# A four-layer graph network on one core: each kind of operation gets its own shift in the planned order

## The chip, the cores and the metric

The kernel runs on one core of a Trainium2 chip. The metric is the device time of one execution in microseconds (us), given as the median of several. The core has a matmul engine (TensorE, in the profile PE, with PEld for the loading of its stationary operand), a vector engine (VectorE, DVE), a scalar engine (ScalarE, ACT), a general engine (GpSimd, POOL) and a queue engine (SyncE, SP), which here issues every DMA. Each engine works through its own instructions in the order in which the program lists them, and waits on semaphores where one needs what another engine has made.

## The reference

128 graphs of 64 nodes with 512 features each: x is (128, 64, 512) and goes through four layers, all with the same 64 x 64 adjacency. Each layer is added to its input and normalized.

```
x = layernorm(x + gnn(x))        # out = deg * (x Wi + b) + adj @ (x Wj)
x = layernorm(x + gat_ffn(x))    # 4 heads, elu, a fifth attention over W_out, elu,
                                 # relu(out @ w1 + b1) @ w2 + b2 + out, layernorm with gamma, beta
x = layernorm(x + gat2(x))       # Wh = x W; e = src_i + dst_j; leaky relu; mask; softmax; attn @ Wh
x = layernorm(x + gat3(x))
```

In a graph attention a score for each pair of nodes (e) is made from two numbers per node (f), masked, turned into weights by a softmax, and these weights average the nodes' rows.

## The kernel before

**Tiling.** The 8192 rows are cut into 32 pairs of two tiles of 128 rows (T = 2, NP = 32); a tile holds two graphs. Every pair passes through the stages of all four layers, and several pairs are under way at a time, each in another layer: a new one is begun every TURN. The names in the profile carry no pair number, but in the text axp_5_1 is pair 5, tile 1.

**Stages.** `stage_first` (line 844) aggregates x over the adjacency on PE (axp, with `aggr` as the moving operand, 64 rows of the array at a time), ACT copies the result to ax, and the product with the first layer's weight follows (l for the first four pairs, stx_0/sty_0 later); POOL adds the row degb = deg * b to x. `stage_scores` (894) makes the heads' scores: for pairs 0 and 1 by PE from x1T (fp), later by DVE's row products j. Its attention (`attention_heads`, 732) is a chain: dg on DVE, bc on PE, the softmax with e on DVE and ACT, the transposition pt on PE, the copies aT on ACT. Then come the four groups yp of eight matmuls (two halves q of the heads, two tiles), again with 64 rows each, and ACT's copies ys; POOL makes the differences t1, t2 of ys and one into ys itself. `stage_heads` (964) multiplies ys with the four heads' weights (stx_h, sty_h) into hT, with elu after it. `stage_project` (1001) multiplies hT with W_out in two halves (stx_o, sty_o) into who. `stage_out` (1041) has the fifth attention (names with 1o; op applies it, in 64 x 64 tiles), the transposition oTp, the two products of the feed-forward part (hidp, then stx_y and sty_y) and the norm with gamma (ng). `stage_gat` (1095) is run for the third and the fourth layer (bc, e, pt, then gp, the copies gT, and stx/sty with W2 or W3); `stage_last` and `stage_tile` do the last pair tile by tile, with plain products (yp of w_last, z) in places.

**Products.** `seven` and `strassen` (611, 663) compute a 2 x 2 block product with seven block products instead of eight. Each is a short unbroken group of matmuls into one of two accumulators: stx (x in the code) or sty (y and z). Their weights are blocks and differences of blocks (11, 21, 12, 22, T1 to T4), read by SP into rings of buffers, ws (4) for two weights and wk (6) for the others.

**The order.** Calls on `nc` aren't emitted but recorded: `Plan.note` (220 and around) makes a `Step` for each call, or for each group within `together()`, with a rank, which is the number in which it was recorded, less 1000 within `soon()`. `Plan.order` then lists the steps by a simulation of its own: for each engine it takes, among the steps whose inputs are there by its own cost estimates, the one with the lowest rank. SLACK and WAIT say how long after its end another engine sees a step. `Plan.play` emits the instructions in that order. So all instructions carry the line of `play` (L314), and a rank matters only against other steps that are ready on the same engine at the time. Buffers are given out in the order of recording, so a step that is to open a buffer waits for an earlier one's to come free. The steps are recorded by a queue of generators, each `yield` giving a stage's next due time.

Of the kernel before, what the change touches and what calls it, by code (L numbers as in the profile page):

```python
# [39 lines left out]

WAIT = 0.2
NEAR = 160
SLACK = {"tensor": 0.8, "sync": 0.4}


class Slots:


    def __init__(self, n):
        self.free, self.queue = [(0.0, i, None) for i in range(n)], []  # L50
        self.openers = []
# [26 lines left out]
class View:  # L78
# [48 lines left out]
    def real(self):  # L127
        a = self.tile.make()
        for name, args, kw in self.steps:
            a = getattr(a, name)(*args, **kw)  # L130
        return a
# [10 lines left out]
class Step:  # L142
    def __init__(self, engine, rank):
        self.engine, self.rank = engine, rank
        self.calls, self.after, self.behind, self.port = [], set(), set(), False
        self.opens, self.uses = [], set()
        self.takes, self.lands = 0.0, 0.0


class Plan:  # L150
# [23 lines left out]
    def note(self, engine, name, args, kw):  # L174
        if self.joined:
            s = self.joined[0]
            assert s.engine == engine
        else:
            s = Step(engine, len(self.steps) - self.early)
            self.steps.append(s)  # L180
            if self.joined is not None:
                self.joined.append(s)
        out = [kw[k] for k in ("out", "accum_out") if k in kw] + (
            [] if "out" in kw or not args else [args[0]]
        )
        views = [(v, True) for v in out if isinstance(v, View)] + [
            (v, False)
            for v in [*args, *kw.values()]
            if isinstance(v, View) and not any(v is o for o in out)
        ]  # L190
        for v, writes in views:
            t = v.tile
            writes = writes or t.pool.space is PSUM
            if not t.seen:
                s.opens.append(t)
            else:
                s.behind.add(t.seen[0][0])
            s.uses.add(t)
            s.after.update(o for o, r, w in t.seen if (w or writes) and v.meets(r))
            t.seen.append((s, v.region, writes))  # L200
        s.after.discard(s)
        s.behind -= {s} | s.after
        s.calls.append((name, args, kw))
        takes, s.lands = cost(engine, name, args, kw, out)
        if engine in ("vector", "gpsimd"):

            both = [v for v, writes in views if not writes and v.tile.pool.space is not PSUM]
            s.port = len(both) > 1 and (engine == "vector" or size_of(out) > 2)
        s.takes += takes

    def order(self):
# [21 lines left out]
        def late(s, e):  # L233
            return 0.0 if s.engine == e else WAIT + SLACK.get(s.engine, 0.3)

# [73 lines left out]
    def play(self):  # L309
        real = lambda v: v.real() if isinstance(v, View) else v  # L310
        with self.tc.manual_schedule():
            for s in self.order():
                for name, args, kw in s.calls:
                    getattr(getattr(self.tc.nc, s.engine), name)(  # L314
                        *map(real, args), **{k: real(v) for k, v in kw.items()}
                    )
# [10 lines left out]
def size_of(out):  # L327
    return max(math.prod(v.shape[1:]) for v in out) if out and isinstance(out[0], View) else 512


def cost(engine, name, args, kw, out):

    size = size_of(out)
    if engine == "tensor":
        if name == "transpose":
            return size * 0.00085, 0.0

        beside = P * P // math.prod(kw["lhsT"].shape)
        return (
            size * 0.00169 if beside == 1 else 0.208 / beside + 0.0003 * size  # L340
        ), 0.0
    if engine == "sync":
        return 0.06, 0.0015 * size
    if name == "tensor_tensor_reduce":
        return 0.7, 0.0
    if engine == "gpsimd":
        return 0.2 + 0.0021 * size, 0.0
    return 0.17 + (0.0011 if engine == "vector" else 0.00085) * size, 0.0
# [1001 lines left out]
```

## Time and profile before

| | us |
|---|---|
| median of three runs | 3346.63 |
| lowest, highest | 3344.84, 3348.06 |
| the profiled execution | 3347.62 |
| its span (first to last instruction) | 3345.8 |
| PE busy within it | 3284.4 |
| DVE, POOL, ACT busy | 2420.4, 1684.7, 1363.8 |

The profile is that of one execution; 1.8 us of its time lie outside the span, and it took 1.0 us longer than the median. PE's busy time counts an instruction as busy from its start to a modelled end; a stretch of busy PE therefore says that it was never without work, not that the work was done as fast as it could be. Most matmuls leave two records in the trace: the x8 of a line stands for four matmuls. The time of a group is read from its start to the start of the next. L314 stands for all of the program; the groups are told apart by the names of their tiles, first the one that is written, then those that are read.

The twelve costliest rows of the page are matmuls and weight loads of the block products, ACT's copies of hT and DVE's row products; no single row has more than a fifth of the span.

### The profile page before, as it was taken

The page shows a single profiled execution, that of the slowest core. Times are in us where ns is not written, and L with a number is a line of the kernel's source. Part 1 is how long each engine was busy: PE and PEld are TensorE (multiplying, and loading weights), DVE is VectorE, ACT ScalarE, POOL GpSimd, SP SyncE. Part 2 cuts the span into 40 slices and gives each one's busy share as a digit, 9 for nine tenths or more (in the row PEclk, how much of TensorE's full clock was granted, in tenths as well). Part 3 has the DMA queues.
Part 4 walks back from the last instruction along what each step waited for, and adds up shares of the span by engine and source line. Part 5 has one row for each costly group of instructions (what it writes and reads, how often), then busy time and mean ns, then how long its engine had stood idle before and what let it go on. Part 6 is the DMA issues. An engine that isn't in the chain of part 4 may idle for free.

```text
span 3345.8 us, 59820 instructions
## 1 busy us (share of the span) xinstructions
PE 3284.4 (98%) x21298; PEld 2888.7 (86%) x21298; DVE 2420.4 (72%) x5698; ACT 1363.8 (41%) x3196; POOL 1684.7 (50%) x1860
## 2 busy tenths in 40 slices
PE   8999999999999999999999999999999999999997
PEld 4888888988988988989888989889889889888884
DVE  5477677777777777777777777777777777777756
ACT  2444344444444443443443443434444444444332
POOL 6745345554455554455554555544555544555442
PEclk9999999999999999999999999999999999999998
DMA  8956656667666666666666666676666666666752
GB/s 309 323 168 199 216 197 215 214 212 235 203 216 218 215 215 224 200 224 215 217 226 213 200 224 218 210 232 204 209 220 216 217 228 201 217 217 208 243 183 66
DMA packets 301062, 718.08 MB, mean 215 GB/s; under 512 B 32560, under 2 KB 41824, under 8 KB 300768
## 3 DMA queue, kind: packets, MB, share of 16 engines
q1 hardware_dynamic: 300768, 714.27, 64.9%
q8 instruction: 171, 2.80, 0.3%
q14 instruction: 123, 1.01, 0.1%
HBM read 680.82 MB, written 33.32 MB: 213 GB/s over the span
## 4 chain that ended last, share of the span: by engine, by line
PE 93%; DVE 2%; DMA 2%; POOL 2%; issue 1%; ACT 0%; SPq 0%; POOLq 0%; DVEq 0%
PE stx_h L314 13%; PE stx_o L314 13%; PE stx L314 12%; PE sty_h L314 10%; PE sty_o L314 10%; PE sty L314 9%; PE hidp L314 5%; PE yp L314 4%; PE gp L314 3%; PE stx_y L314 3%; PE sty_y L314 2%; PE axp L314 2%; PE bc L314 1%; DMA rows<-d_h 1%; PE op L314 1%; PE l L314 1%
## 5 line engine op out<-in xcount | busy, mean ns | idle before, releaser
L314 DVE CUSTOM_DVE_ANT_0 j<-x,rows 128x512 bf16<-128x512 f32 x736 | 627.9, 853 | 53.5 <-DMA rows<-d_h 23.0
L314 PEld LDWEIGHTS stx_h<-ys,wh 128*128 128x128 f32 x3072 | 392.0, 192 | 16.3 <-issue 0.9
L314 PE MATMUL stx_h<-ys,wh 128*128 128x128 f32 x3072 | 404.7, 275 | 1.1 <-DVE r_1o L314 0.8
L314 ACT COPY hT<-stx_h 128x256 f32<-128x256 f32 x384 | 142.9, 373 | 480.1 <-PE stx_h L314 335.8
L314 POOL TENSOR_SCALAR rs<-mv 128x1 f32<-128x1 f32 x256 | 70.8, 277 | 501.9 <-DVE mv L314 492.0
L314 ACT ACTIVATE x<-x,sh,rs 128x512 f32<-128x512 f32 x256 | 209.1, 817 | 203.8 <-DVE sh L314 202.9
L314 PE MATMUL sty_h<-ys,wh 128*128 128x128 f32 x2048 | 274.0, 277 | 2.8 <-ACT hT L314 2.8
L314 POOL TENSOR_TENSOR ys<-ys,t 128x256 f32<-128x256 f32 x128 | 114.5, 896 | 302.2 <-PE sty_h L314 302.0
L314 PEld LDWEIGHTS sty_h<-ys,wh 128*128 128x128 f32 x2048 | 249.6, 192 | 7.9 <-ACT hT L314 3.7
L314 PE MATMUL stx_o<-ws_wo_T,s_o 128*128 128x256 f32 x1024 | 246.1, 383 | 3.6 <-ACT who L314 2.7
L314 PE MATMUL sty_o<-ws_wo,hT 128*128 128x256 f32 x1024 | 242.4, 380 | 2.5 <-DMA ws_wo<-d_wo 2.5
L314 PE MATMUL hidp<-oT,w 128*128 128x256 f32 (+1 forms) x1056 | 231.1, 373 | 0.0
L314 DVE TENSOR_TENSOR hT<-sty_h,hT 128x256 f32<-128x256 f32 x256 | 107.9, 422 | 150.1 <-PE sty_h L314 146.8
L314 PEld LDWEIGHTS hidp<-oT,w 128*128 128x128 f32 x1056 | 193.5, 190 | 24.9 <-issue 0.5
L314 PEld LDWEIGHTS sty_o<-ws_wo,hT 128*128 128x128 f32 x1024 | 190.0, 190 | 27.1 <-DMA ws_wo<-d_wo 2.7
L314 DVE TENSOR_TENSOR x<-stx,x 128x256 f32<-128x256 f32 x360 | 149.2, 420 | 87.1 <-PE stx L314 83.6
L314 PEld LDWEIGHTS stx_o<-ws_wo_T,s_o 128*128 128x128 f32 x1024 | 186.0, 191 | 28.8 <-ACT who L314 3.6
L314 DVE SCALAR_TENSOR_TENSOR hT<-elu,hT 128x512 f32<-128x512 f32 x256 | 174.8, 684 | 40.6 <-ACT elu L314 37.1
L314 ACT ACTIVATE elu<-hT 128x512 f32<-128x512 f32 x256 | 153.7, 601 | 70.0 <-DVE hT L314 66.7
L314 DVE BATCH_NORM_STATS2 st<-x 128x6 f32<-128x512 f32 x256 | 177.0, 691 | 5.5
L314 ACT COPY ys<-yp 128x512 f32<-128x512 f32 x256 | 131.7, 600 | 114.1 <-PE yp L314 113.2
L314 DVE TENSOR_TENSOR x<-sty,x 128x512 f32<-128x512 f32 (+1 forms) x180 | 100.1, 556 | 87.2 <-PE sty L314 84.1
(201 smaller groups left out, 7719.3 us busy)
## 6 DMA issues: line engine op xcount, KB each, us to landing
ws_wo_T<-d_wo_T SPq DMA_DIRECT2D x256, 512.0 KB, 3.7
ws_wo<-d_wo SPq DMA_DIRECT2D x192, 512.0 KB, 3.9
ws_W_T<-d_W_T SPq DMA_DIRECT2D x248, 256.0 KB, 3.6
rows<-d_h SPq DMA_DIRECT2D x240, 256.0 KB, 4.7
ws_w_T<-d_w_T SPq DMA_DIRECT2D x112, 512.0 KB, 3.3
ws_W<-d_W SPq DMA_DIRECT2D x186, 256.0 KB, 3.7
ws_w<-d_w SPq DMA_DIRECT2D x84, 512.0 KB, 4.1
rows<-d SPq DMA_DIRECT2D x128, 256.0 KB, 4.8
```

Of the source, the lines that this page charges most:

```text
L314: getattr(getattr(self.tc.nc, s.engine), name)(*map(real, args), **{k: real(v) for k, v in kw.items()})
```

## The change

SLACK of the matmul engine goes from 0.8 to 0.691. Each step gets a kind when its first call is recorded: two letters of its engine, and the name of the tile that it writes without the numbers ("te:bc": a matmul into a bc). Before the order is made, `play` adds to a step's rank what the table LATER has for its kind, and for its kind in its part of the program: S is the first 11% of the recorded steps, E the last 7%, M the rest (for which the table has no entry). A positive number sends a step behind others that are ready, a negative one ahead. The table has 26 entries for 23 kinds on the four computing engines and SP. No operation is added, removed or changed.

```diff
-SLACK = {"tensor": 0.8, "sync": 0.4}
+SLACK = {"tensor": 0.691, "sync": 0.4}
+LATER = {
+    "gp:bones/S": 40, "gp:fill": 120, "gp:rs": -20, "gp:s_o": -20, "gp:s_o/E": -20, "gp:ys": 8,
+    "sc:x": 100, "sy:w/S": 20, "te:bc": -60, "te:bc_o": 40, "te:fp": -12, "te:hidp": 18,
+    "te:hidp/S": 20, "te:l": -21, "te:pt/E": 9, "te:pt_o/E": -20, "te:stx/S": 80,
+    "te:stx_y/E": 80, "te:stx_y/S": 60, "te:sty_o/E": 4, "te:wap": -100, "ve:abd/S": 23,
+    "ve:deg": 40, "ve:gT/E": -100, "ve:ng": 200, "ve:who/S": -40,
+}
...
         self.calls, self.after, self.behind, self.port = [], set(), set(), False
+        self.kind = ""
...
         s.calls.append((name, args, kw))
+        if not s.kind:
+            what = out[0].tile.args.get("name", "?") if out and isinstance(out[0], View) else "dram"
+            what = re.sub("__+", "_", re.sub(r"\d+", "", what).rstrip("_"))
+            s.kind = f"{engine[:2]}:{what}"
...
         with self.tc.manual_schedule():
+            n = len(self.steps)
+            for i, s in enumerate(self.steps):
+                when = "S" if i < 0.11 * n else "E" if i > 0.93 * n else "M"
+                s.rank += LATER.get(s.kind, 0) + LATER.get(f"{s.kind}/{when}", 0)
             for s in self.order():
```

## The prediction

> **What bounds the kernel now.** I read the page first, then the waits of the matmul engine, then busy time by windows, then the timeline of one steady pair and of the places with gaps. The page:
>
> ```profile
> span 3345.8 us, 59820 instructions
> PE 3284.4 (98%) x21298; PEld 2888.7 (86%) x21298; DVE 2420.4 (72%) x5698; ACT 1363.8 (41%) x3196; POOL 1684.7 (50%) x1860
> ...
> PEclk9999999999999999999999999999999999999998
> ...
> PE 93%; DVE 2%; DMA 2%; POOL 2%; issue 1%; ACT 0%; SPq 0%; POOLq 0%; DVEq 0%
> ```
>
> PE is idle for 3345.8 - 3284.4 = 61.4 us in all, and the chain of waits runs on PE for 93% of the span. Nothing but PE's own time and these 61 us can be won. The windows (PE busy, weight loads, DVE, ACT, POOL, granted clock, DMA share, GB/s) say where the idle time lies:
>
> ```profile
> 0.00:107.00 107.00, 91.95 (x444) 54.58 (x445) 59.63 (x131) 31.37 (x60) 70.39 (x73) 0.92 0.89 313
> ...
> 428.00:535.00 107.00, 103.46 (x711) 92.09 (x713) 78.45 (x187) 46.25 (x109) 53.58 (x62) 0.98 0.60 195
> 535.00:636.20 101.20, 101.20 (x671) 90.34 (x669) 71.10 (x177) 43.11 (x101) 50.88 (x56) 1.00 0.69 223
> ...
> 3210.00:3346.00 136.00, 107.27 (x486) 78.75 (x484) 82.31 (x231) 39.84 (x108) 39.33 (x64) 0.90 0.36 120
> ```
>
> The first five windows of 107 us have about 30 us of idle PE, the last 136 us have 28.7, and the 2675 us between have 2.9. There a pair takes 101.2 us with PE full. So the middle can only become shorter if the same matmuls take less PE time. The waits (total, times, longest) name what is late at both ends:
>
> ```profile
> PE pt L314 <- DVE e L314: 8.2, 5, 4.3
> PE bc L314 <- DVE dg L314: 5.7, 1, 5.7
> PE abd_ps L314 <- DVE abd L314: 4.9, 1, 4.9
> ...
> PE sty_h L314 <- ACT hT L314: 2.8, 5, 0.7
> ...
> PE sty_o L314 <- DMA ws_wo<-d_wo: 2.5, 1, 2.5
> ```
>
> The first is the attention's DVE chain, the third the first microseconds, the fourth the only wait of the middle. PE's timeline in a steady pair (start, length, matmuls):
>
> ```profile
> 1033.67 1.24 PE L314 MATMUL stx_o<-ws_wo_T,s_o 128*128 128x256 f32 x5
> 1034.84 2.06 PE L314 MATMUL yp<-aT,x 64*128 64x128 f32 x32
> 1036.82 1.13 PE L314 MATMUL stx_y<-ws_w_T,hid 128*128 128x256 f32 x4
> 1037.79 1.89 PE L314 MATMUL sty_o<-ws_wo,hT 128*128 128x256 f32 x8
> 1039.61 2.06 PE L314 MATMUL yp<-aT,x 64*128 64x128 f32 x32
> 1041.60 1.16 PE L314 MATMUL sty_h<-ys,wh 128*128 128x128 f32 x8
> ```
>
> Each matmul leaves two records, and lengths overlap, so starts are to be subtracted. Elsewhere four stx_y records go from start to start in 0.86 and eight sty_o in 1.73. Beside a yp group stx_y takes 36.82 to 37.79 = 0.97, and sty_o ahead of one 37.79 to 39.61 = 1.82. One group of eight axp matmuls (1026.64 to 1027.73) takes 1.09, two groups of eight yp (1034.84 to 1036.82) 1.98, four of them unbroken (from 436.57 in the timeline) 3.77. With 0.89 for a group, each fits n x 0.89 + 0.20. So one unbroken segment of 64-row matmuls costs 0.10 on the way in, 0.20 inside, 0.10 on the way out: about 0.40 us, however long it is.
>
> **What the Trainium skill says.** "TensorEngine Tiling (Array Packing)", section "Tiling Modes", states "Mode switching requires drain". yp, axp and op use 64 rows, all else 128; the 0.40 above is this trace's price of it. "TensorE: Matmul & The Clock Gate", Part 1 on the HAM clock gate, has the array's clock fall to half after an idle window of some 3.4 us. The trace agrees in kind, and already at shorter gaps: after the gap of 4.25 us at 430.87 eight records of sty take 2.78 instead of 1.73, the next eight 2.46. "SBUF — State Buffer", section on its two sides, says that DVE with two SBUF inputs and GpSimd lock each other out. In the first 90 us a DVE sh of 0.16 us lasted 2.29 beside a POOL addition. "Perfetto Trace Analysis", section "Identifying the Most-Contended Engine", warns that PE's busy share is not its efficiency: here too PE is "full" while the segments cost time in it.
>
> **The change part by part.** The instructions of each engine are the same in kind and number; only their order changes. Put side by side, the two orders give four effects.
>
> 1. *Merged yp segments.* A pair has four yp groups of eight matmuls (stage_scores' aggregation). Before, they stand in two segments for 27 pairs, as in the timeline, and in 66 segments in all; after, with bc 60 ranks earlier, hidp 18 later and POOL's subtraction into ys 8 later, in one for 28 pairs, and in 38 in all. axp (60) and op (33, then 32) stay. 28 x 0.40 = -11.2 us, of it 0.4 in each steady pair, so 100.8 there.
>
> 2. *Start, 0 to 107 us.* deg and degb come before aggr on DVE, so the first axp no longer starts at 6.18 but when b0's DMA is in. That took 6.3 us from its issue at 4.03; now it stands ahead of the w0 tiles on SP, so 7.6 to 10.3, plus 0.5 for degb, plus aggr: 9.3 to 10.5, or +3.1 to +4.3 on PE. PE then runs through to 59.8, where it waits 2.12 for wap_h, which hangs on the chain of weight sums (POOL, DVE, DMA), not on PE, and loses 2.1 us at half clock afterwards. That covers the delay: PE arrives later at the same wait. At the next gap (5.68 before bc at 89.74, chain of x_1's norm) fp and bc change places and dg stands behind other work: -1 to +1. I take 0, with -2 to +4.
>
> 3. *Early pairs, 107 to 535 us.* Distances in PE work between what hands to DVE and what waits for it: bc_3_0 to pt_3_0 3.52 before, 7.82 after; pt_3_0 to gp3_0 0 and 2.62; pt_3_1 to gp3_1 0 and 3.46. The gaps at these places (1.16, 0.73, 0.84) go: -2.7. For the 4.25 gap before pt at 430.87, `ng` 200 ranks later takes foreign instructions out of the e_1_4 chain on DVE: 16 of 5.76 us before, 8 of 3.41 after (-2.35), and 0.87 us more PE work lies between: -3.2 of 5.1 (with the 0.85 gap ahead of it), and some -1.5 of the half clock's 1.8. wo0's T tiles are loaded earlier on SP: the 0.90 gap at 136 goes. The 2.73 at 192 stays (the copy of who is still behind elu on ACT). Sum -8.3; I take -8, with -2 to -11, as each new place could have its own wait.
>
> 4. *Tail, 3210 to 3346.* stx_o and sty_o stand so that the 2.45 us wait for ws_wo at 3218 has 0.8 us more work ahead of it: -1. The first yp of the last pair stands earlier, pulling that tile's attention by 2 to 3 us, but oTp of pair 31 stands nearer its o (a possible wait of 1 to 1.5). After gp the two orders are nearly the same, and the chain bc, e, pt, gp of DVE and PE stays. -2.5, with +2 to -7.
>
> The rest of the middle moves without a price as long as distances suffice. The shortest one: the last ys-dependent product. Before, 4.40 us of PE work lie between the first yp half and sty_h of head 0; merged, 1.81. ACT's four copies take 0.55 to 0.6 each and start 1.16 after the first yp, so the fourth ends 3.4 after it; sty_h stands at 3.76. Slack 0.35 us. The other rings keep their distances (ws tiles 9.8 us of PE work from slot to use, wk 5.3; loads took 3.3 to 4.1). sty_h's five waits of the middle behind hT (2.8 in all), which follow late row loads, may go or grow: 0, with -3 to +3.
>
> Sum: -11.2 + 0 - 8 - 2.5 + 0 = -21.7. The span becomes 3345.8 - 21.7 = 3324.1. The profiled run was 3347.62, 1.8 above its span and 1.0 above the median: 3324.1 + 1.8 - 1.0 = 3324.9, so 3325.
>
> **The rivals.**
> *A: only the segments count.* Start and tail are chains over several engines: what is taken out of one wait is late at the next (the 2.73 at 192 and the tail's chain are unchanged). -11.2 and -1: 3334. For it: chains through DVE are only moved; against: the 4.25 gap has 2.35 us of other DVE work in it that does go.
> *B: the ends recover in full.* -11.2, early -11, start -2, tail -7, and three of the small waits: -34, so 3312. For it: the half clock after gaps, which makes each shortened gap count nearly twice; against: the later axp at the start.
> *C: slower.* ACT isn't free when yp begins. One norm (x, 0.81 us) and one ax copy (0.57) ahead of the ys copies make the fourth late by 0.81 + 0.57 - 0.35 = 1.0; with a second norm 1.8 us. For 28 pairs at 1.8, +50 - 22 = +28: 3375; at the 1.0, +6: 3353. It decides from 21.7 / 28 = 0.8 us a pair. For it: ACT's timeline in this pair shows a norm at 1032.21 and ax copies to 1034.1, right ahead; against: ACT was then idle for 1.90 us before the first ys, and is busy for 41%. Taken at 3356.
> *D: nothing.* Half of the gain of 1 given back in waits of a quarter of a microsecond and the ends as before: about 3342. The order of the middle does change on all engines, so "not done" is excluded; a balance isn't.
>
> **How the numbers follow.** Forecast 0.50 (its own range 3317 to 3331), A 0.23, B 0.13, D 0.08, C 0.06. Two runs of this kernel can't tell less than 0.2%, 6.7 us, from no change, so faster is below 3339.9 and slower above 3353.3. Forecast, A and B are faster, with a little of D: 0.88. Most of D and a part of C are the same: 0.07; the rest of C: 0.05. The range 3309 to 3341 leaves out C, most of D and the far side of B, about 0.15.
>
> **What would show it.** Right: yp x64 in one segment of 3.77 in the steady pairs and a period near 100.8; first axp at 9 to 10.5 with wap_h's gap gone or below 1; no gap of 4 us near 430; about 45 us of idle PE in place of 61. Wrong: gaps before sty_h on ACT's ys in each pair (C); a period still at 101.2, which would mean that the 0.40 isn't a price of the segment; gaps moved, not gone, in the first 535 us (A); a wap_h gap that stays after a later axp (+4).

## The result, and the profile after

The changed kernel takes 3316.47 us (median of four runs, 3314.83 to 3322.36) against 3347.35 us for the kernel before (four runs too, 3344.84 to 3350.77), a ratio of 0.991 with a 95% interval of 0.9893 to 0.9927. The forecast was 3325 us with a range of 3309 to 3341: the result lies inside the range, 8.5 us below the forecast. The span of the profiled execution went from 3345.8 to 3313.0 us, 32.8 us less where the forecast's sum was 21.7.

The page of the kernel after, its first lines and the chain of waits by engine:

```profile
span 3313.0 us, 59778 instructions
PE 3266.4 (99%) x21298; PEld 2886.0 (87%) x21298; DVE 2491.0 (75%) x5698; ACT 1362.8 (41%) x3196; POOL 1714.9 (52%) x1860
...
PE 94%; DMA 3%; DVE 1%; POOL 1%; SPq 1%; issue 0%; ACT 0%; POOLq 0%; DVEq 0%; ACTq 0%
```

Idle PE fell from 61.4 to 3313.0 - 3266.4 = 46.6 us: 14.8 us of the gain are waits that are gone. The other 18.0 us are busy PE that became shorter, with the same matmuls. This is the split of one execution. The run without deg (below) has the same order but for one short DVE instruction in the first 5 us, so it is in effect a second profile of the changed kernel: a span of 3312.7 us, and 10.2 and 22.9 us in place of 14.8 and 18.0.

Where the 32.8 us lie is read from windows that are cut at the same work in both kernels: at the start of yp of the pairs 6, 28 and 30. Columns: window and its length, busy time of PE, weight loads, DVE, ACT and POOL (with instructions), granted clock, DMA share, GB/s. First the kernel before:

```profile
0.00:630.00 630.00, 599.87 (x3789) 506.12 (x3789) 421.70 (x981) 245.61 (x563) 335.37 (x349) 0.98 0.70 233
630.00:2860.10 2230.10, 2228.05 (x14677) 1989.32 (x14676) 1657.68 (x3894) 930.23 (x2178) 1130.80 (x1255) 1.00 0.66 216
2860.10:3063.60 203.50, 202.78 (x1335) 180.81 (x1334) 151.44 (x354) 84.48 (x198) 103.05 (x115) 1.00 0.67 215
3063.60:3345.80 282.20, 253.67 (x1502) 212.50 (x1501) 189.61 (x469) 103.46 (x257) 115.49 (x144) 0.95 0.50 165
```

and the kernel after:

```profile
0.00:618.30 618.30, 598.34 (x3809) 509.43 (x3809) 432.93 (x987) 246.08 (x563) 346.01 (x353) 0.98 0.72 239
618.30:2839.40 2221.10, 2220.08 (x14677) 1988.30 (x14676) 1715.79 (x3894) 928.45 (x2178) 1153.05 (x1255) 1.00 0.67 217
2839.40:3042.10 202.70, 202.09 (x1337) 180.69 (x1336) 155.02 (x354) 84.39 (x198) 105.66 (x115) 1.00 0.67 216
3042.10:3313.00 270.90, 245.87 (x1482) 207.59 (x1481) 187.25 (x463) 103.86 (x257) 110.21 (x140) 0.96 0.52 168
```

The four stretches are shorter by 11.7, 9.0, 0.8 and 11.3 us. In the long one the number of matmul records is the same, so it compares directly: 22 pairs, 0.41 us each; of the 9.0 us, 1.03 are waits and 7.97 busy PE. The first stretch does 20 records more after the change than before, the last 20 fewer: some stx_o, sty_o and stx_y groups now run before that cut instead of at the end. At the 0.216 us from one of these records to the next, this is 4.3 us of work. So the first stretch really won 11.7 + 4.3 = 16.0 us, the last 11.3 - 4.3 = 7.0. The first figure is rough: three runs below that keep this order up to pair 6 (those without E, without sc:x and without deg) reach its yp 9.7, 11.3 and 14.6 us ahead of the kernel before, where this execution has 11.7. The last stretch is steadier, with 271.0 us in the run without deg where this execution has 270.9.

In a steady pair of the kernel after, PE's timeline (start, length, group of matmuls) has the yp groups in one piece:

```profile
1929.92 1.89 PE L334 MATMUL stx_o<-ws_wo_T,s_o 128*128 128x256 f32 x8
1931.74 3.84 PE L334 MATMUL yp<-aT,x 64*128 64x128 f32 x64
1935.51 1.16 PE L334 MATMUL sty_h<-ys,wh 128*128 128x128 f32 x8
```

From 1931.74 to 1935.51 are 3.77 us. From one pair's yp to the next pair's are 100.81 us in 11 of the 24 pairs from 6 to 29, and never less; before, the shortest period was 101.21, in 16 of 24. The waits of PE in the kernel after (total, times, longest):

```profile
...
PE bc L334 <- DVE dg L334: 4.4, 1, 4.4
PE bc L334 <- DVE r L334: 4.1, 1, 4.1
PE axp L334 <- DVE aggr L334: 3.9, 1, 3.9
...
PE stx_o L334 <- ACT who L334: 2.7, 1, 2.7
PE sty_y L334 <- DMA ws_w<-d_w: 2.4, 6, 0.8
PE pt L334 <- DVE e L334: 2.2, 3, 1.8
```

The 8.2 us of pt behind e have become 2.2, the sty_h waits of the middle are gone, and six short waits of sty_y for a weight tile are new (2.4 us, on the ring that the moved groups share). DVE's busy time rose by 70.6 us, nearly all of it in j (627.9 us before, 694.6 after, with the same 736 instructions). It cost nothing visible, as PE was full. All of it lies in the j that run beside an instruction of POOL: 445 of them took 0.96 us on average before, 444 take 1.11 after, while the others take 0.69 in both.

### The profile page after: what moved, and what is told of

The parts are those of the page before. It is cut to its first block, busy times and chain, and to the rows that moved or that the text cites. A ratio compares the mean times of both kernels' runs of the same rounds, so it can differ in the third digit from the quotient of the medians.

```text
span 3313.0 us, 59778 instructions
## 1 busy us (share of the span) xinstructions
PE 3266.4 (99%) x21298; PEld 2886.0 (87%) x21298; DVE 2491.0 (75%) x5698; ACT 1362.8 (41%) x3196; POOL 1714.9 (52%) x1860
## 3 DMA queue, kind: packets, MB, share of 16 engines
q14 instruction: 123, 1.01, 0.1%
## 4 chain that ended last, share of the span: by engine, by line
PE 94%; DMA 3%; DVE 1%; POOL 1%; SPq 1%; issue 0%; ACT 0%; POOLq 0%; DVEq 0%; ACTq 0%
PE stx_h L334 14%; PE stx_o L334 13%; PE stx L334 12%; PE sty_h L334 11%; PE sty_o L334 10%; PE sty L334 9%; PE hidp L334 7%; PE yp L334 4%; PE gp L334 3%; PE stx_y L334 3%; PE sty_y L334 2%; PE axp L334 2%; PE bc L334 1%; DMA ws_w<-d_w 1%; PE op L334 1%; PE oTp L334 1%
## 5 line engine op out<-in xcount | busy, mean ns | idle before, releaser
L334 DVE CUSTOM_DVE_ANT_0 j<-x,rows 128x512 bf16<-128x512 f32 x736 | 694.6, 944 | 75.2 <-ACT x L334 42.5
L334 PEld LDWEIGHTS stx_h<-ys,wh 128*128 128x128 f32 x3072 | 383.6, 192 | 14.2 <-issue 1.6
L334 POOL TENSOR_TENSOR ys<-ys,t 128x256 f32<-128x256 f32 x128 | 122.6, 966 | 200.6 <-PE sty_h L334 198.0
L334 DVE SCALAR_TENSOR_TENSOR sh<-mv,rs 128x1 f32<-128x1 f32 x256 | 120.8, 472 | 101.6 <-POOL rs L334 101.4
L334 ACT COPY ax<-axp 128x512 f32<-128x512 f32 x128 | 68.6, 589 | 300.3 <-PE axp L334 298.9
```

Source lines behind the costliest of these rows:

```text
L334: getattr(getattr(self.tc.nc, s.engine), name)(*map(real, args), **{k: real(v) for k, v in kw.items()})
```

## The experiments

All are edits of the kernel after unless stated. With four executions the interval of a ratio reaches some 5 us to either side, so a smaller difference between two medians isn't clear of noise; there the profile has to decide.

**SLACK alone.**

```diff
-LATER = {
-    "gp:bones/S": 40, "gp:fill": 120, "gp:rs": -20, ...
-}
+LATER = {
+}
```

> Only SLACK 0.691; the table of shifts is empty. Its order has 47 yp segments (66 before, 38 after). Theory 'kinds': the shifts make both the merging of yp and the shorter ends, SLACK is a detail: then this run is no better than its count, 19 segments x 0.40 = -7.6, so about 3340 with the ends' 61 us of idle PE as before. Rival 'slack': SLACK alone does most of the change: about 3320, a steady period of 100.8 us and idle PE near 47 us.

Measured: 3346.93 us, ratio 1.0004 (0.9996 to 1.0013): no gain at all, worse than both expectations. The profile shows why it isn't simply "nothing happened". At yp of pair 6 this run was 8.7 us ahead of the kernel before (the changed kernel 11.7). In the middle the pairs don't settle: yp stands in one piece in some, in two in others, with periods of 100.8 us only from pair 22 on and new waits of sty_h for POOL's t, of sty_y and stx_y for weight tiles. At pair 30 the lead is 5.8 us where the changed kernel has 21.6. The tail then loses all of it: its waits sum to 27.4 us against 20.3 in the kernel before, the longest 4.6 for DVE's sh. So SLACK can bring the early gain and the merging, but without the shifts neither is kept.

**The shifts alone.**

```diff
-SLACK = {"tensor": 0.691, "sync": 0.4}
+SLACK = {"tensor": 0.8, "sync": 0.4}
```

> All 26 shifts, SLACK back at 0.8. Its order has 64 yp segments. Theory 'segments': with the yp groups split again the steady period is 101.2 us as before (not 100.8), and only the ends' gain remains: of the 32.8 us of span some 11 are lost, about 3327. Rival 'the shifts shorten the middle in another way': period 100.8, about 3317. Rival 'slack': the ends go back too, 3345.

Measured: 3337.64 us, 0.9978 (0.997 to 0.9986). The period is 101.21 in the steady pairs, as the first theory has it: with 64 segments there is no shorter middle. But the ends gained less than expected: 6.1 us up to pair 6, with 27.5 us of idle PE in the first 500 us where the changed kernel has 19 to 22. Each half alone is worth 0 and 7 us, both together 31, so the two don't add up. Each can change what is ready when the other decides; which decisions those are wasn't traced.

**The price of a segment.** A pass over the finished order moves one later group into the middle of each yp segment:

```diff
-            for s in self.order():
+            for s in self.cut(self.order()):
...
+            if j - i > 2:
+                half, place = pe[(i + j) // 2], {s: k for k, s in enumerate(out)}
+                for x in pe[j : j + 30]:
+                    if (
+                        x.kind[3:6] in ("stx", "sty") and not x.opens
+                        and all(place[o] < place[half] for o in x.after | x.behind)
+                    ):
+                        out.remove(x)
+                        out.insert(place[half], x)
+                        break
```

> After, with one later stx or sty group (mostly stx_o) moved between the second and third yp group of each segment: 27 segments more, nothing else moved. Theory 'a segment costs 0.40 us': +10.8 us, 3327, and a steady period of 101.2. Rival 'the saved time isn't the segment's but that of the neighbours' order': within 2 us of after, 3316 to 3318. More than 3335 would be a new wait, of the moved group for its weights.

Measured: 3331.35 us, 0.996 (0.9946 to 0.9974), 14.9 above the kernel after. PE's timeline in a steady pair of this run:

```profile
1942.56 2.06 PE L353 MATMUL yp<-aT,x 64*128 64x128 f32 x32
1944.54 1.99 PE L353 MATMUL stx_o<-ws_wo_T,hT 128*128 128x256 f32 x8
1946.46 2.06 PE L353 MATMUL yp<-aT,x 64*128 64x128 f32 x32
1948.45 1.16 PE L353 MATMUL sty_h<-ys,wh 128*128 128x128 f32 x8
```

The pieces take 1.98 and 1.99 us, the group between them 1.92 instead of 1.73. Together that is 5.89 where one piece and the same group apart take 3.77 + 1.73 = 5.50: 0.39 us. And the shortest and commonest period is 101.21 again, to the hundredth that of the kernel before. The 0.40 us is the segment's price. The total is larger than 27 x 0.40 = 10.8: the spans of the two profiled executions differ by 17.8 us. Of this, 2.4 were lost before the first yp, where the two orders are the same, and 11.2 in the 22 pairs of the long stretch, where the segments explain 8.8. Where the rest comes from isn't shown.

**Joining more.** If that is so, the two axp groups of a pair, which stood apart, are worth joining too:

```diff
+    "te:axp/M": 60,
```

> After, with one more shift: axp 60 ranks later between start and end (te:axp/M: 60). In its order the two axp groups of a pair stand directly ahead of the four yp groups: 48 segments of axp and yp where after has 98. Theory 'a segment costs 0.40 us': 50 x 0.40 = -20.0, a steady period of 100.0 us (two segments fewer, -0.8) and about 3297. Rival 'axp is needed where it stood': ax comes some 12 us later, the sums of POOL and the first layer's products wait, PE gets gaps in each pair and the time is 3316 or more.

Measured: 3352.59 us, 1.002 (1.0012 to 1.0027): slower than the kernel before. The rival had it right that something waits in each pair, but not what. PE's timeline in a steady pair of this run:

```profile
1949.46 2.06 PE L356 MATMUL axp<-aggr,x 64*128 64x128 f32 x32
1951.35 3.74 PE L356 MATMUL yp<-aT,x 64*128 64x128 f32 x64
1955.02 1.16 PE L356 MATMUL sty_h<-ys,wh 128*128 128x128 f32 x8
...
1959.71 1.16 PE L356 MATMUL sty_h<-t,wh 128*128 128x128 f32 x8 [1.75 <-POOL t L356]
```

The joined segment takes 5.56 us, which is 6 x 0.89 + 0.20 = 5.54. So the segment did what it was to do: PE's busy time is 3253.6 us, 12.8 less than after the change. But the wait in brackets comes 24 times, 41.8 us in all. POOL's timeline of the same stretch names what stood ahead of t:

```profile
1955.36 1.28 POOL L356 TENSOR_TENSOR s<-ax 128x512 f32<-128x512 f32 x1
1956.71 1.27 POOL L356 TENSOR_TENSOR s<-ax,s 128x512 f32<-128x512 f32 x1
1957.94 1.71 POOL L356 TENSOR_TENSOR t<-ys 128x512 f32<-128x512 f32 x1
```

The two sums s run first, though what reads them next, POOL's own ax<-ax,s, starts only 13 us later, at 1970.88.

**The same with POOL's order mended.** A pass over the finished order puts these two sums behind t1, t2 and ys:

```diff
-            for s in self.order():
+            for s in self.hold(self.order()):
...
+                for x in [x for x in pool[max(i - 5, 0) : i] if x.kind == "gp:s"][::-1]:
+                    a, b = out.index(x), out.index(pool[i + 2])
...
+                        out.insert(b + 1, x)
+                        out.remove(x)
```

> As the run with axp joined to yp, and in addition the two sums s of the next pair's first layer stand behind t1, t2 and ys on POOL instead of ahead of them. Theory 'the joined segments are worth 0.40 each, and the loss there was POOL's t alone' (41.8 us of waits of sty_h): the waits go, the steady period is 100.0 to 100.3 us and the time 3297 to 3305, the fastest of all. Rival 'another wait takes its place' (ys copies of ACT, or ax): period 101 or more, 3320 or more.

Measured: 3306.62 us (3305.68 to 3309.65), 0.9887 (0.9871 to 0.9904): the fastest of all, 9.9 us below the changed kernel by the medians and some 8 by the ratios, a little above the expected 3297 to 3305. The period is 100.02 to 100.05 us in half of the pairs (100.0 expected). On every engine but POOL the order is that of the run with axp joined, so POOL's order alone makes the difference of some 45 us. POOL now has:

```profile
1933.36 1.27 POOL L371 TENSOR_TENSOR t<-ys 128x512 f32<-128x512 f32 x1
1934.71 1.27 POOL L371 TENSOR_TENSOR t<-ys,t 128x512 f32<-128x512 f32 x1
1935.94 1.71 POOL L371 TENSOR_TENSOR ys<-ys 128x512 f32<-128x512 f32 x1
1937.61 1.72 POOL L371 TENSOR_TENSOR s<-ax 128x512 f32<-128x512 f32 x1
```

Most of what is missing to 3297 is lost in the pairs 4 to 6, where axp passes from its old place to the new one: four waits of 0.7 to 1.5 us, and a lead over the kernel before of 5.9 us at pair 6 where the changed kernel has 11.7 (9.7 to 14.6 in its repeats). Another 3.4 us go in the part after yp of pair 30 (274.3 us, 270.9 in the changed kernel), 2.1 of them in a longer wait for ws_wo.

**Start and end.** The shifts for the end removed, then those for the start, then both:

```diff
-    ... every entry with "/E"
```

> After without the six shifts for the end (E). 37 yp segments. Theory 'the E shifts shorten the tail': the tail's gain of some 7 us beyond the forecast's step 4 goes, 3322 to 3324, and the idle PE of the last 135 us returns from 25 to 28.5. Rival 'the tail is shorter through what comes before it and the shifts that hold everywhere': 3316 to 3318.

```diff
-    ... every entry with "/S"
```

> After without the seven shifts for the start (S). 37 yp segments. Theory 'the start's gain comes from the S shifts': the 15 us that are won up to pair 6 shrink by half or more, 3324 to 3330. Rival 'it comes from the shifts that hold everywhere (ng, deg, rs) and SLACK', as SLACK alone already reached pair 4's yp 19.9 us earlier: 3316 to 3320.

```diff
-    ... every entry with "/S" or "/E"
```

> After with the thirteen shifts that hold everywhere and SLACK 0.691, without those for start and end. 36 yp segments. Theory 'parts add up': after plus what the runs without S and without E each lost, 3324 to 3328. Rival 'S and E only repair each other's damage': 3316 to 3320. Rival 'nothing holds without S and E': over 3335, as with SLACK alone.

Measured: 3321.64 (0.993, 0.9912 to 0.9948), 3321.09 (0.993, 0.9915 to 0.9945) and 3326.77 us (0.9948, 0.9933 to 0.9963), that is 5.2, 4.6 and 10.3 us above the kernel after. The parts add up within the noise, as expected of the third run. Of the 31 us, 17 to 21 belong to SLACK with the thirteen shifts that hold everywhere, and some 5 each to start and end, though by the times alone each 5 is no larger than the interval. The profile makes the E part sure, at half the size of the first theory: without E the part after yp of pair 30 takes 274.4 us, and without S and E 274.2, where the changed kernel takes 270.9. In both, sty waits 1.20 us for DVE's gT and z 2.04 and 0.73 for ACT's. How much of the early gain is the S shifts' stays open. Without S the lead at pair 6 is 9.7 us, without S and E it is 2.2, and the two orders are the same up to there, so a single execution can't tell. In both, three waits at pair 4 that the changed kernel doesn't have are there: 0.95, 0.41 and 1.27 us.

**Single shifts.** Four were removed one at a time: "ve:deg": 40, "ve:ng": 200, "sc:x": 100 and "te:bc": -60.

> After without the shift of deg and degb. Theory 'the later axp is covered by the wait for wap_h' (step 2): the first axp starts near 6.2 again, PE waits about 2 us for wap_h near 62, and the time is within 2 us of after: 3315 to 3319. Rival 'the later start costs': 3 us faster, 3312 to 3314. Rival 'the wait brings the half clock, which costs more than the later start': 3318 to 3320.

Measured: 3316.98 us (0.992, 0.9903 to 0.9936). The run doesn't test what it was made for: the shift holds for deg alone, degb is another kind, and axp started at 8.97, as in the changed kernel. The run without S tests it, see below. As a repeat of the changed kernel it is of use all the same.

> After without the shift of ng (DVE, 200 ranks later). 36 yp segments. Theory 'ng's shift takes the foreign DVE work out of the e_1_4 chain' (step 3): a gap of 2 to 4 us ahead of pt near 425 returns with its half clock, +4 to +6: 3320 to 3323. Rival 'the distances on PE alone close that gap': no gap there, 3315 to 3318. ng also shifts DVE in every pair: if it holds the middle together, new gaps in the middle and more than 3325.

Measured: 3321.14 us (0.9932, 0.9917 to 0.9947). The wait of pt for e is back at 421.11 with 1.97 us, after one of 1.45 for who; the lead at pair 6 is 7.8 us instead of 9.7 to 14.6. The theory holds, at its lower end; none of the four profiles with the shift and the rest of the changed kernel's early order has this wait.

> After without the shift of ACT's norms (sc:x, 100 ranks later). 38 yp segments. In the tail before, ACT stood at a norm of x that waited 2.9 us for DVE's sh, with the copy of gT for PE behind it. Theory 'this shift removes that wait': PE waits again for a gT copy near the end, with the half clock after it: +3 to +5, 3320 to 3322. Rival 'the tail's order on PE already takes the copy out of the way': 3315 to 3319, no such wait.

Measured: 3317.55 us (0.9917, 0.9902 to 0.9932), and a wait of sty for ACT's gT of 0.26 us alone, where the kernel before has 2.48: the rival.

> After without the shift of the heads' and gat's bc (te:bc, 60 ranks earlier), which the forecast named as one cause of the merged yp. 36 yp segments in its order. Theory 'the merging comes from SLACK together with no single shift': period 100.8 us all the same and 3315 to 3322. Rival 'bc earlier keeps the attention's DVE chains covered': new waits of pt for e, over 3325.

Measured: 3322.07 us (0.993, 0.9914 to 0.9947). The period is 100.81 without this shift, so it doesn't make the merging. What it did hold is the place in pair 4, where pt waits 1.97 us again.

## Why the prediction was right or wrong

**Step 1, merged segments: right in size, with a cause that isn't enough.** Forecast: 28 segments fewer, 0.40 us each, a period of 100.8. Measured: a period of 100.81, 9.0 us in 22 pairs, and the run with the segments cut has 101.21 again. The forecast named bc, hidp and ys as what moves the groups together. The runs show that these aren't enough: all 26 shifts with the old SLACK give 101.21, and leaving bc out gives 100.81. SLACK is needed, and by itself, with an empty table, it merges part of the pairs (47 segments). bc isn't needed; hidp and ys weren't removed singly, so their part stays open.

**Step 2, start: right.** Forecast: first axp at 9.3 to 10.5, covered by the wait for wap_h, net 0. Measured in DVE's timeline of the kernel after (start, length):

```profile
7.91 0.49 DVE L334 TENSOR_SCALAR degb<-degb,deg 128x512 f32<-128x512 f32 x1 [3.08 <-DMA degb<-in_b_dram]
8.31 0.45 DVE L334 COPY aggr<-abd_ps 64x64 f32<-64x64 f32 x2
```

and axp at 9.10, 2.9 later than before, with no wait for wap_h. In the run without S, aggr stood ahead of degb again and axp started at 6.21, but the wait for wap_h was back with 1.32 us, and the first yp came at 91.95 against 92.30. Three microseconds at the start were worth 0.35 here. Net, the changed kernel is 1.2 us ahead at the first yp. Both differences are within what one execution differs from the next: the same order up to there reaches the first yp between 92.3 and 94.6 us in the four profiles that have the changed kernel's early order, and at 91.9 and 93.7 in the two without. The net of 0 stands, to about a microsecond.

**Step 3, early pairs: the mechanism right, the sum too small.** Forecast -8, and with three merged segments about -9.2 up to pair 6. Measured: -16.0, of it 1.2 before the first yp, and some 2 to 3 us to either side from one execution to the next. The waits that were counted as going did go (4.25, 1.16, 0.84, 0.73, 0.90 and the 0.85 in front of the first), the one counted as staying, 2.73 at 192, stayed. But four small ones that the sum left in place went too: 0.35, 1.09, 0.26 and 0.68, together 2.4 us. And part of the half clock that was kept after the gaps as an uncertain extra was recovered: l keeps PE busy for 57.3 us instead of 58.9, and sty in this stretch 41.4 instead of 43.1, with the same records. How much half clock a gap brings differs from one execution to the next, as the last section shows, so this part of the gain is partly luck. The forecast's example of a slowdown after a gap shorter than the idle window that it cites, the gap of 4.25, is longer than that window; the gap of 2.12 before 61.93 is shorter and shows it, with a granted clock of 0.50 from 63.4 to 66.7. That the gain at pair 4 hangs on more than one shift is shown by the runs without ng and without bc: in each a wait of 1.97 comes back there.

**Step 4, tail: the term that was mis-sized.** Forecast -2.5, with one merged segment -2.9; measured -7.0. The wait for ws_wo went the way that was forecast (2.45 to 0.66; 1 was taken). Missed was a wait that the forecast had put down as part of a fixed chain: "after gp the two orders are nearly the same". In the kernel before, PE's timeline there:

```profile
3284.13 1.13 PE L314 MATMUL sty<-ws_W,gT 128*128 128x256 f32 x4 [2.48 <-ACT gT L314]
3285.10 1.49 PE L314 MATMUL stx<-ws_W,gT 128*128 128x256 f32 x4
3286.44 0.47 PE L314 MATMUL bc<-ident,f 128*128 128x128 f32 x1
3286.78 2.07 PE L314 MATMUL sty<-ws_W_T,gT 128*128 128x256 f32 x4
3288.64 1.18 PE L314 MATMUL stx<-ws_W_T,s 128*128 128x256 f32 x4
3289.95 1.10 PE L314 MATMUL sty<-ws_W,gT 128*128 128x256 f32 x4
```

gp was done by 3281.6, yet gT came at 3284. ACT's timeline says why:

```profile
3282.66 0.81 ACT L314 ACTIVATE x<-x,sh,rs 128x512 f32<-128x512 f32 x1 [2.88 <-DVE sh L314]
3283.49 0.86 ACT L314 COPY gT<-gp 128x512 f32<-128x512 f32 x2
```

The copy stood behind a norm that waited for DVE's sh. PE lost 2.48 us and then, with four groups and a bc taking 3284.13 to 3289.95 = 5.82 us instead of 4 x 0.86 + 0.11 = 3.55, another 2.3, most of it at a granted clock of 0.50 (3285.5 to 3288.9). In the kernel after the copy runs as soon as gp is done:

```profile
3251.32 0.59 ACT L334 COPY gT<-gp 128x512 f32<-128x512 f32 x1 [1.07 <-PE gp L334]
```

Which shift does it isn't settled. It isn't sc:x, whose removal brought nothing back, nor the E shifts alone, since without them sty's wait for this copy doesn't return either. The gain here is partly spent on new waits of 1.26 and 0.73 for the same groups and a longer one of gp (0.73 to 1.36): from gp to the next pt, 13.44 us (3279.60 to 3293.04) have become 11.23 (3250.07 to 3261.30). So of the 7.0 us, 2.2 are won here, 1.8 at ws_wo, and 1.0 by an op group that is no longer split (last section); the other 2 weren't taken apart.

**The rest of the middle** was taken as 0, with -3 to +3. The five sty_h waits went, six sty_y waits came: -1.03 in the long stretch.

**Rivals.** A (3334) and D (3342) are out. B (3312, the ends recover in full, as the half clock makes a shortened gap count nearly twice) came nearer to the measured time than the forecast, and its -7 for the tail is what was measured; it deserved more than 0.13. Its reason holds in part only: four small waits and the copy of gT went too, and the half clock doesn't follow every gap. C, a wait of sty_h in each pair behind an engine that is held up by other work, didn't come about in the changed kernel: ACT had been idle for 2.9 us when its first ys copy could start. But the run with axp joined shows that this mechanism is real and of the size feared, on POOL instead of ACT: 1.75 us in each of 24 pairs, enough to lose more than everything.

## What to carry to other kernels

On an engine that is full, look for time inside its busy time: here the change from 128-row to 64-row matmuls and back cost 0.4 us each time, and grouping them was worth 0.4 us a pair and, carried further, 1.2. An engine that works strictly in order should have the next wanted result ahead of what merely is ready first: the two sums on POOL decided between the slowest and the fastest kernel of this study. And when parameters of a planner change together, test them apart before crediting any of them: one half brought 0 us, the other 7, both 31. Before a few microseconds of one stretch are put down to a change, a second profile of the same order should be looked at: here two of them were 2.9 us apart by pair 6.

## What the runs showed of the hardware that wasn't expected

**The half clock after a wait has no fixed price.** In the kernel after and in the run without deg, PE comes to the same wait of 2.73 us with the same order. First the kernel after, then the run without deg (timeline, then the window of these eight records; the granted clock is the third number from the end):

```profile
189.93 3.78 PE L334 MATMUL stx_o<-ws_wo_T,s_o 128*128 128x256 f32 x8 [2.73 <-ACT who L334]
189.93:193.50 3.57, 3.57 (x8) 2.75 (x9) 3.54 (x8) 0.37 (x1) 2.65 (x2) 0.50 0.00 0
```

```profile
190.03 1.99 PE L354 MATMUL stx_o<-ws_wo_T,s_o 128*128 128x256 f32 x8 [2.73 <-ACT who L354]
190.03:191.86 1.83, 1.83 (x8) 1.58 (x9) 1.83 (x6) 0.00 (x0) 1.75 (x2) 1.00 0.00 0
```

The same eight records take 3.57 us at a granted clock of 0.50, and 1.83 at 1.00. Twelve profiles of this study have this wait, with 2.73 or 2.74 us; behind it the eight records take 1.83 us in two of them, 2.24 to 3.22 in three, and 3.57 or 3.58 in seven. So one execution of an order can lose here what the next doesn't. What decides it wasn't tried.

**Split op groups.** The op groups, 64 x 64 matmuls for the two tiles of a pair, took as long for four records as for eight. Before, in the tail, they stood apart, at 3253.38 and 3255.45, and took 1.01 and 1.00 us with four records each; after, at 3227.91, all eight took 1.02. One more separate piece of op thus cost a full microsecond, more than twice a yp segment. The records show how: of the eight, four start within 0.02 us of each other and overlap in full, and 0.46 us later the other four do; of a piece of four records, two start together, and 0.47 us later the other two. In the whole group four run side by side, in a piece only two, in the same time.
